# Two attention layers on one core: even batches and merged sums in layer 0, a direct first chunk, sums by query rows at the end

## The chip, the core and the metric

The kernel runs on one core of a Trainium2 chip, as one program. TensorE (PE, with its weight loads PEld), VectorE (DVE), ScalarE (ACT), GpSimd (POOL) and SyncE (SP) run beside each other, each through its own queue of instructions; transfers are issued from the queues of SP, ACT and POOL. The metric is device microseconds (us) of an execution.

## The reference

For each of 8 images of 64 channels and 64 x 64 points (N = 4096 points), two attentions follow each other:

```python
# layer 0
f = Wf @ x + bf;  g = Wg @ x + bg;  hh = Wh @ x + bh     # 8, 8 and 64 channels
beta = softmax(f.T @ g, axis=2)                          # 4096 x 4096
x = x + hh @ beta.T
# layer 1
xn = group_norm(x, 8 groups) * gamma + beta
q, k, v = split(w_qkv @ xn + b_qkv)
attn = softmax(q.T @ k / 8)
x = x + w_proj @ (v @ attn.T) + b_proj
```

All of it is float32.

## The kernel before

**Tiles.** An image stands in 128 rows: 64 channels of the first half of the points, 64 channels of the second half, 2048 columns each. A chunk `c` is 512 query points in each half, so an image has 4 chunks in each layer. For one chunk, a step `t` (16 of them) takes 128 key points, in both halves `p` of the keys, against both halves `h` of the queries. That is four score matmuls of 512 columns, here called units, which fill four of the eight PSUM banks; ScalarE takes the exponential into a tile `e` (128 x 2048; six buffers, tag `e` of `ppool`); TensorE multiplies `e` with the values (`weigh`), and VectorE adds `e` to `esum` (line 662), of which the softmax sums are made. A part is one key half of a step: two units. The softmax has no shift by a maximum: `bounds` looks at the end whether any sum left a safe range, and a flag read by the engines chooses a general path if one did.

**Layer 0.** f and g have 8 channels, each kept in four groups of 32 rows (one group for each pair of `h` and `p`), split into a high and a low part so that scores run in the float32r format. `project(k)` makes chunks 2k and 2k+1 of f and g at once: matmuls into one pair of banks, one activation that adds the bias (line 417), a cast into `high` (line 419), the split (line 422), and then 16 transfers on SP (line 432) that put the parts into their rows of f and g. `full` and `high` have one buffer each. `values(c)` makes the values of a chunk; outside of the loop VectorE copies them (line 298), within it ScalarE does.

**Layer 1.** Scores and weighing use 64 x 64 tiles of the array; a step is two pairs of banks. Group norm of image b's layer 1 and its q, k and values are made in earlier steps, as are f, g and values of later images.

**Order.** Chunks run in the order layer 0 of image 0, layer 0 of image 1, layer 1 of image 0, layer 0 of image 2, layer 1 of image 1, and so on. TensorE's order is exactly that of the program (`in_order`, line 137 is the matmul helper); on the other engines the framework orders by readiness, within given constraints (`issue_after`). Other work is put in by step number (`at_step`, `take`): work that takes a pair of banks (PAIR) or one spare bank (BANK) at most once in a batch.

**A batch of layer 0** is one turn of the loop: it scores as many units as there are free banks, 6, or 7 where the outer bank is free (`closed == 0`), 2 fewer where a PAIR is taken; then TensorE weighs parts whose exponentials were made in earlier batches. `due_part` lets it weigh up to 7 units' worth, 3.5 parts (a part can be cut into two halves of 256 columns), whatever the batch scored.

**The end of a chunk** (`finish`): the accumulated output is copied to `raw`. In layer 1, VectorE then adds the two halves of `esum` (line 312), and four matmuls with a block of ones (`sums`, some steps later) give the sums of 256 columns each; in layer 0 there is no such addition, the four matmuls have 512 columns, and the two halves are added after the sums were laid out (line 345). The sums go to `zs` (line 331), by four transfers to `zt` with 128 rows, through a reciprocal (line 347), to memory and back as a row for all channels (`r`), and `raw` is multiplied by it (line 366). The very last chunk has a short cut, `at_once`: two matmuls with ones give the sums in all rows, then a reciprocal of 128 x 512 (line 361), the product, the residual and `bounds` (lines 796 to 802).

**The start.** SP loads image 0 in four transfers of 64 rows; ACT's queue loads the weights of f and g in four transfers (line 169), POOL's the biases, `wh` and the small constants. All of `before()` of image 0 runs ahead of the loop: both projections with their 32 transfers, and the values of all four chunks. Then SP loads images 1 and 2, behind those transfers.

Of the kernel before, what the change touches and what calls it, by code (L numbers as in the profile page):

```python
# [9 lines left out]
F32 = mybir.dt.float32  # L10
# [58 lines left out]
def fast_path(  # L69
# [69 lines left out]
    x_tiles = {}  # L139

    def load_x(b):
        t = xpool.tile([P, NH], F32, tag="x", name=f"x_{b}")
        for k in range(2):
            for h in range(2):
                nc.sync.dma_start(
                    t[ts(h, C), ts(k, NH // 2)], x[b, :, ds(h * NH + k * (NH // 2), NH // 2)]
                )
        x_tiles[b] = t

    def both(name, src):  # L150
        t = const.tile([P, 1], F32, name=name)
        for h in range(2):
            nc.gpsimd.dma_start(t[ts(h, C), :], column(src))
        return t
# [6 lines left out]


    load_x(0)

    w1 = const.tile([P, 2, C8], F32, name="w1")
    fgb = const.tile([P, 1], F32, name="fgb")
    for h in range(2):
        for i, (w, bias) in enumerate(((WfT, bf), (WgT, bg))):
            nc.scalar.dma_start(w1[ts(h, C), i, :], w)  # L169
            nc.gpsimd.dma_start(  # L170
                fgb[ts(2 * h + i, 4 * C8), :], bias.unsqueeze(0).broadcast_to([4, C8])
            )
    wfg = const.tile([P, 2, 4, C8], F32, name="wfg")
# [3 lines left out]
    lane, low = const.tile([P, 1], I32, name="lane"), const.tile([P, 1], I32, name="low")  # L177
    nc.gpsimd.iota(lane, pattern=[[0, 1]], base=0, channel_multiplier=1)
    nc.vector.tensor_scalar(  # L179
        low, lane, 1, 2 * C8, op0=ALU.logical_shift_right, op1=ALU.bitwise_and  # L180
    )
    nc.vector.tensor_tensor(low, low, lane, op=ALU.bitwise_and)
    nc.vector.tensor_single_scalar(low, low, 1, op=ALU.logical_shift_right)
    nc.vector.tensor_tensor(low, low, lane, op=ALU.bitwise_xor)
    nc.vector.tensor_single_scalar(low, low, C8, op=ALU.bitwise_and)
    lowmask = const.tile([P, 1], F32, name="lowmask")
    nc.vector.tensor_scalar(lowmask, low, -1.0 / C8, None, op0=ALU.mult)
    wh = twice("wh", WhT)
# [20 lines left out]
    gavg = gavg.rearrange("p h g s -> p (h g s)")  # L209

# [7 lines left out]
    def layer1_constants():  # L218
# [20 lines left out]
        bet = both("bet", beta)  # L239
        wvt = const.tile([C, 2, C], F32, name="wvt")  # L240
# [957 lines left out]
```

## Time and profile before

| what | value |
|---|---|
| median of 3 runs | 3106.06 us (3105.13 to 3106.15) |
| profiled execution | 3105.83 us, span of its instructions 3104.1 us |
| TensorE busy | 3063.5 us (99%) |
| VectorE busy | 2506.6 us (81%) |
| ScalarE busy | 2045.5 us (66%) |
| mean granted TensorE clock | 0.996 of full speed |

The profile is of one execution. Times in it count from the first instruction of the span. A row of a group gives line, engine, operation, what it writes and reads, shapes and count, then busy time and mean duration of one in ns, then idle time of the engine ahead of them with what ended it. A row of the order of time gives start, duration, engine, line and what was done, with equal neighbours put together. One float32 matmul shows as two matmul records. TensorE's busy share tells little by itself, as its matmuls overlap; the time from the start of one row to the start of the next is the better measure.

### The profile page before, as it was taken

Reading aid. Unit: us, or ns where it says so; the run is one execution under the profiler, and the core shown is the slowest. Engines: PE = TensorE matmul, PEld = TensorE weight load, DVE = VectorE, ACT = ScalarE, POOL = GpSimd, SP = SyncE. Lnnn points to the kernel's source line nnn. Section 1 sums busy time; section 2 is a strip of 40 time slices with the busy share of each in tenths; the row PEclk is TensorE's granted clock in tenths of the full one; section 3 lists DMA queues with packets and bytes.
Section 4 is the critical chain, followed back from the end, with each engine's and each line's share of the span. In section 5 each row is a group of like instructions: output and inputs, shape, how many; then the busy total and the mean of one; then the engine's idle time right before and its main releaser. Section 6 shows DMA issues by size and latency. Waiting matters only on the chain.

```text
span 3104.1 us, 58905 instructions
## 1 busy us (share of the span) xinstructions
PE 3063.5 (99%) x25863; PEld 1122.5 (36%) x25863; DVE 2506.6 (81%) x1616; ACT 2045.5 (66%) x1976; POOL 16.7 (1%) x41
## 2 busy tenths in 40 slices
PE   7999999999999999999999999999999999999998
PEld 2333334333343333433334333343334333334433
DVE  6999876898768987689877997779977799776666
ACT  5788655786557865578555785558855587555554
POOL 2000000000000000000000000000000000000000
PEclk9999999999999999999999999999999999999999
DMA  3000010100101001010011000100001000000000
GB/s 84 22 8 11 18 39 15 32 1 15 39 21 26 1 15 39 22 25 1 15 39 25 21 1 19 42 19 21 1 25 35 19 8 2 14 22 15 10 13 12
DMA packets 61816, 63.16 MB, mean 20 GB/s; under 512 B 34944, under 2 KB 35024, under 8 KB 61552
## 3 DMA queue, kind: packets, MB, share of 16 engines
q1 hardware_dynamic: 60432, 59.16, 7.8%
q8 instruction: 204, 3.34, 0.5%
q14 instruction: 60, 0.49, 0.1%
q0 software_dynamic: 800, 0.15, 0.0%
q10 hardware_dynamic: 320, 0.01, 0.0%
HBM read 25.06 MB, written 8.65 MB: 11 GB/s over the span
## 4 chain that ended last, share of the span: by engine, by line
PE 96%; DVE 1%; ACT 1%; issue 1%; SPq 0%; DMA 0%; ACTq 0%; DVEq 0%
PE banks L137 96%; DVE esum_l L662 1%; ACT e_l L776 1%; SPq L432 0%; ACT e_l L736 0%; DMA w<-in_WgT_dram 0%; DMA x<-in_x_dram 0%; DVE vt_l L298 0%; DVE r_l L361 0%; DVE high_l L422 0%; DMA fg_l<-high_l 0%; ACTq L169 0%; DVE raw_l L366 0%; DVE esum_l L312 0%; ACT full_l L417 0%
## 5 line engine op out<-in xcount | busy, mean ns | idle before, releaser
L662 DVE TENSOR_TENSOR esum_l<-esum_l,e_l 128x2048 f32<-128x2048 f32 x896 | 2052.4, 2291 | 473.2 <-ACT e_l L736 414.5
L736 ACT ACTIVATE e_l<-banks 128x1024 f32<-128x1024 f32 x1024 | 992.8, 1021 | 802.8 <-PE banks L137 770.1
L137 PE MATMUL banks<-e_l,v_l 64*64 64x512 f32 (+1 forms) x8744 | 1098.5, 589 | 0.0
L776 ACT ACTIVATE e_l<-banks 128x2048 f32<-128x2048 f32 (+3 forms) x768 | 955.7, 1310 | 213.1 <-PE banks L137 207.9
L137 PE MATMUL banks<-kq_l 64*64 64x512 f32 (+1 forms) x8448 | 1010.2, 586 | 1.2 <-ACT e_l L776 1.1
L137 PE MATMUL banks<-e_l,vt_l 128*64 128x512 f32 (+1 forms) x3884 | 831.5, 567 | 0.0
L137 PEld LDWEIGHTS banks<-e_l,v_l 64*64 64x64 f32 (+1 forms) x8744 | 360.0, 133 | 576.0 <-issue 534.0
L137 PEld LDWEIGHTS banks<-kq_l 64*64 64x64 f32 (+1 forms) x8448 | 348.7, 134 | 579.3 <-issue 544.6
L137 PEld LDWEIGHTS banks<-e_l,vt_l 128*64 128x64 f32 x3884 | 254.3, 136 | 470.4 <-issue 457.0
L137 PE MATMUL banks<-fg_l 32*128 32x512 f32 x1792 | 220.2, 465 | 10.7 <-ACT e_l L776 5.7
L662 DVE TENSOR_TENSOR esum_l<-e_l,e_l 128x2048 f32<-128x2048 f32 x64 | 146.5, 2288 | 48.4 <-ACT e_l L736 35.9
L137 PEld LDWEIGHTS banks<-fg_l 32*128 32x128 f32 x1792 | 92.1, 183 | 219.4 <-ACT e_l L776 134.8
L137 PE MATMUL banks<-esum_l,ones 128*32 128x512 f32 (+2 forms) x508 | 55.2, 501 | 4.4 <-DVE esum_l L312 2.7
L568 DVE COPY raw_l<-banks 128x512 f32<-128x512 f32 x32 | 22.1, 692 | 31.3 <-PE banks L137 31.3
L366 DVE TENSOR_TENSOR raw_l<-raw_l,r_l 128x512 f32<-128x512 f32 x64 | 43.8, 684 | 0.0
L542 ACT ACTIVATE kq_l<-banks,qkb 128x512 f32<-128x512 f32 x64 | 40.6, 696 | 0.0
L312 DVE TENSOR_TENSOR esum_l<-esum_l 128x1024 f32<-128x1024 f32 x32 | 38.9, 1216 | 0.0
L137 PE MATMUL banks<-xn_l,wqk 64*64 64x512 f32 x256 | 33.4, 592 | 0.0
L331 ACT COPY zs_l<-banks 128x512 f32<-128x512 f32 (+1 forms) x63 | 30.9, 491 | 0.0
L137 PE MATMUL banks<-x,wfg 64*64 64x512 f32 x128 | 19.0, 640 | 9.7 <-DVE low L179 9.3
L137 PEld LDWEIGHTS banks<-wh,x 64*64 64x64 f32 x1024 | 22.0, 135 | 15.7 <-issue 13.3
L137 PEld LDWEIGHTS banks<-wvp,xn_l 64*64 64x64 f32 x1024 | 20.6, 134 | 16.8 <-issue 16.8
(89 smaller groups left out, 378.2 us busy)
## 6 DMA issues: line engine op xcount, KB each, us to landing
r_l<-recips SPq DMA_DIRECT2D x126, 128.0 KB, 2.9
fg_l<-high_l SPq DMA_DIRECT2D x224, 64.0 KB, 2.0
x<-in_x_dram SPq DMA_DIRECT2D x32, 256.0 KB, 5.2
kq_l<-kq_l SPq DMA_DIRECT2D x64, 128.0 KB, 2.3
out_dram<-raw_l SPq DMA_DIRECT2D x64, 128.0 KB, 2.4
kq_l<-high_l SPq DMA_DIRECT2D x32, 64.0 KB, 2.0
zt_l<-zs_l SPq DMA_DIRECT2D x128, 2.0 KB, 1.8
zt_l<-zs_l SPq DMA_DIRECT2D x124, 1.0 KB, 1.7
```

The costliest lines, as they stand in the source:

```text
L137: in_order(nc.tensor.matmul(*args, **kwargs))
L312: nc.vector.tensor_add(esum[:, 0], esum[:, 0], esum[:, 1])
L331: nc.scalar.copy(zs, z[:, 0:width])
L366: nc.vector.tensor_mul(raw, raw, r)
L542: nc.scalar.activation(self.parts[:, h, cols], ps[:, h, :], AF.Identity, bias=k1["qkb"][:, h : h + 1],)
L568: nc.vector.tensor_copy(raw, acc[0])
L662: added = nc.vector.tensor_add(esum, first if t == 1 else esum, e).ins
L736: nc.scalar.activation(e[:, p], both_ps[p], AF.Exp, scale=at.scale)
L776: nc.scalar.activation(e.rearrange("k p h n -> k (p h) n")[:, first_ : first_ + n_, :], banks[:, bank : bank + n_, :], AF.Exp, scale=at.scale,
```

## The change

Six edits. (1) `due_part` gets the room to weigh as the batch's own number of units: 7, 6, or 2 fewer. (2) Layer 0 adds the halves of `esum` on VectorE, right behind its last addition, and its sums have 256 columns as in layer 1. (3) The first chunk of image 0's f and g comes from matmuls with weights that already stand in the rows' layout (`direct`), so that it needs no transfer; the second chunk is projected alone, the third and fourth in step 1 of the loop, the values of chunks 1 to 3 in steps 2, 5 and 8. (4) Image 0 is loaded in three transfers of 128 rows, later images in two; the weights of f and g come in two transfers on ACT's queue, `wh` in one; images 1 and 2 are loaded from POOL's queue behind its small constants. (5) `fgb` and `lowmask` are put together by eight small copies on POOL. (6) In the last chunk the sums come as eight matmuls with `esum` as the weights, which puts queries in rows; the reciprocal is 128 x 8, and eight matmuls with the identity lay it out over the channels.

```diff
-
-    def load_x(b):
+    sent = []
+    def load_x(b, engine, cuts):
         t = xpool.tile([P, NH], F32, tag="x", name=f"x_{b}")
-        for k in range(2):
-            for h in range(2):
-                nc.sync.dma_start(
-                    t[ts(h, C), ts(k, NH // 2)], x[b, :, ds(h * NH + k * (NH // 2), NH // 2)]
-                )
+        for i, j in zip(cuts, cuts[1:]):
+            made = engine.dma_start(
+                t[:, i * CW : j * CW],
+                x[b].rearrange("c (h n) -> h c n", h=2)[:, :, i * CW : j * CW],
+            )
         x_tiles[b] = t
+        return made
     def both(name, src):
         t = const.tile([P, 1], F32, name=name)
         for h in range(2):
-            nc.gpsimd.dma_start(t[ts(h, C), :], column(src))
+            sent.append(nc.gpsimd.dma_start(t[ts(h, C), :], column(src)))
...
-    load_x(0)
-
     w1 = const.tile([P, 2, C8], F32, name="w1")
-    fgb = const.tile([P, 1], F32, name="fgb")
+    for i, w in enumerate((WfT, WgT)):
+        nc.scalar.dma_start(w1[:, i, :], w.unsqueeze(0).broadcast_to([2, C, C8]))
+    load_x(0, nc.sync, (0, 1, 2, 4))
+    bias2 = const.tile([P, 2], F32, name="bias2")
+    for i, bias in enumerate((bf, bg)):
+        nc.gpsimd.dma_start(
+            bias2[:, i : i + 1], bias.unsqueeze(0).broadcast_to([P // C8, C8])
+        )
+    direct = const.tile([P, 2, P], F32, name="direct")
+    nc.vector.memset(direct, 0.0)
     for h in range(2):
-        for i, (w, bias) in enumerate(((WfT, bf), (WgT, bg))):
-            nc.scalar.dma_start(w1[ts(h, C), i, :], w)
-            nc.gpsimd.dma_start(
-                fgb[ts(2 * h + i, 4 * C8), :], bias.unsqueeze(0).broadcast_to([4, C8])
-            )
+        rows = ts(h, C)
+        for i, at, n in ((0, h * C, 8), (1, h * 32, 4), (1, C + h * 32, 4)):
+            nc.vector.tensor_copy(
+                direct[rows, i, at : at + n * C8].rearrange("q (s c) -> q s c", c=C8),
+                w1[rows, i, :].unsqueeze(1).broadcast_to([C, n, C8]),
+            )
     wfg = const.tile([P, 2, 4, C8], F32, name="wfg")
     nc.vector.tensor_copy(wfg, w1.unsqueeze(2).broadcast_to([P, 2, 4, C8]))
     wfg = wfg.rearrange("p i s c -> p (i s c)")
-    lane, low = const.tile([P, 1], I32, name="lane"), const.tile([P, 1], I32, name="low")
...
-    wh = twice("wh", WhT)
+    nc.vector.tensor_tensor(low[:, 1:2], low[:, 0:1], low[:, 1:2], op=ALU.bitwise_xor)
+    lowmask2 = const.tile([P, 2], F32, name="lowmask2")
+    nc.vector.tensor_scalar(lowmask2, low, -1.0 / C8, None, op0=ALU.mult)
+    wh = const.tile([P, C], F32, name="wh")
+    nc.scalar.dma_start(wh, WhT.unsqueeze(0).broadcast_to([2, C, C]))
...
+    fgb, lowmask = const.tile([P, 1], F32, name="fgb"), const.tile([P, 1], F32, name="lowmask")
+    for j in range(2):
+        for i in range(2):
+            rows = ts(2 * j + i, 32)
+            nc.gpsimd.tensor_copy(fgb[rows, :], bias2[rows, i : i + 1])
+            nc.gpsimd.tensor_copy(lowmask[rows, :], lowmask2[rows, i : i + 1])
...
+        with tc.issue_after(sent[-1].ins):
+            for b in (1, 2):
+                load_x(b, nc.gpsimd, (0, 2, 4))
...
             raw = work.tile([P, CW], F32, tag="raw", bufs=4, name=f"raw_{n}")
+            last = index == 2 * B * NC - 1
+            if last:
+                with tc.issue_after(added):
+                    nc.vector.tensor_add(esum[:, 0], esum[:, 0], esum[:, 1])
             copied = self.total(raw, acc)
-            zt = small.tile([P, 2, QP], F32, tag="zt", bufs=5, name=f"zt_{n}")
-            width = CW if self.kind == 0 else CW // 2
-            if self.kind == 1:
-                with tc.issue_after(copied.ins):
+            zt = small.tile([P, QP], F32, tag="zt", bufs=4, name=f"zt_{n}")
+            width = CW // 2
+            if not last:
+                with tc.issue_after(copied.ins if self.kind == 1 else added):
                     nc.vector.tensor_add(esum[:, 0], esum[:, 0], esum[:, 1])
             r = None
...
-                zs = work.tile([P, CW], F32, tag="zs", bufs=1, name=f"zs_{n}")[:, 0:width]
+                zs = work.tile([P, width], F32, tag="zs", name=f"zs_{n}")
                 for h in range(2):
                     for i in range(2):
                         row = 32 * (2 * h + i)
-                        what = esum[:, i, h, :] if self.kind == 0 else esum[:, 0, h, ts(i, width)]
                         matmul(
-                            z[row : row + 32, 0:width], ones[:, 0:32], what,
+                            z[row : row + 32, 0:width], ones[:, 0:32], esum[:, 0, h, ts(i, width)],
                             start=True, stop=True, tile_position=(0, row),
                         )
                 nc.scalar.copy(zs, z[:, 0:width])
                 for h in range(2):
                     for i in range(2):
                         row = 32 * (2 * h + i)
-                        dst = zt[ts(h, C), i, :] if self.kind == 0 else zt[row : row + 32, 0, :]
-                        nc.sync.dma_start(dst, zs[row : row + 1, :])
+                        nc.sync.dma_start(zt[row : row + 32, :], zs[row : row + 1, :])
...
             def reciprocals():
-                zh = zt[:, 0, :]
-                if self.kind == 0:
-                    nc.vector.tensor_add(zh, zh, zt[:, 1, :])
                 rt = stash[:, ts(index, QP)]
-                nc.vector.reciprocal(rt, zh)
+                nc.vector.reciprocal(rt, zt)
                 broadcast()
...
             def at_once():
-                broadcast()
-                z = pair()[:, 0, :]
-                for h in range(2):
-                    matmul(z[ts(h, C), :], ones, esum[:, 0, h, :], start=True, stop=True)
-                nc.vector.reciprocal(r, z)
+                parts = [(h, k) for h in range(2) for k in range(TPC)]
+                z = pair()[:, 0, 0:QP]
+                for i, (h, k) in enumerate(parts):
+                    matmul(
+                        z[:, i : i + 1], esum[:, 0, h, ts(k, P)], ones[:, 0:1],
+                        start=True, stop=True,
+                    )
+                rt = zt
+                nc.vector.reciprocal(rt, z)
+                rows = work.tile([P, QP, C], F32, tag="full", bufs=1, name="rt_rows")
+                nc.vector.tensor_copy(rows, rt.unsqueeze(2).broadcast_to([P, QP, C]))
+                laid = pair()[:, 0, :]
+                for i, (h, k) in enumerate(parts):
+                    matmul(
+                        laid[ts(h, C), ts(k, P)], rows[:, i, :], ident, start=True, stop=True
+                    )
+                bounds(rt, 1)
+                nonlocal r
+                r = laid
                 result()
-                bounds(r, 1)
             def result():
                 nc.vector.tensor_mul(raw, raw, r)
                 self.residual(raw, c)
-            if index == 2 * B * NC - 1:
+            if last:
                 return (at_once,)
             return sums, reciprocals, result
...
-                self.project(0)
-
+                if self.b > 0:
+                    self.project(0)
+            if self.b == 0:
+                xt = x_tiles[0]
+                def first():
+                    begin()
+                    self.project_direct(0)
+                return [(-1, first, True), (-1, lambda: self.project(0, (1,)), True)] + [
+                    (1, lambda: self.project(1), True)
+                ] + [
+                    (
+                        (-1, 2, 5, 8)[c],
+                        lambda c=c: self.values(xt[:, ts(c, CW)], wh, c),
+                        True,
+                    )
+                    for c in range(NC)
+                ]
             at = (12, 28) if self.b == 1 else (17, 26)
             return [(at[0], begin, True), (at[1], lambda: self.project(1), True)] + [
...
-        def project(self, k):
+        def project_direct(self, c):
+            n = f"{self.name}_{c}"
+            cols = ts(c, CW)
+            ps = pair()
+            full = work.tile([P, 2, CW], F32, tag="full", bufs=1, name=f"full_{n}")
+            high = work.tile([P, 2, CW], F32R, tag="high", bufs=1, name=f"high_{n}")
+            for i, dst in enumerate((self.f, self.g)):
+                matmul(
+                    ps[:, i, :], direct[:, i, :], x_tiles[self.b][:, cols], start=True, stop=True
+                )
+                nc.scalar.activation(
+                    full[:, i, :], ps[:, i, :], AF.Identity, bias=bias2[:, i : i + 1]
+                )
+                nc.vector.tensor_copy(high[:, i, :], full[:, i, :])
+                nc.vector.scalar_tensor_tensor(
+                    dst[:, cols], high[:, i, :].bitcast(F32), lowmask2[:, i : i + 1],
+                    full[:, i, :], op0=ALU.mult, op1=ALU.add,
+                )
+        def project(self, k, js=(0, 1)):
             n = f"{self.name}_{k}"
             xt = x_tiles[self.b]
             ps = pair()
-            for j in range(2):
+            for j in js:
                 for h in range(2):
                     matmul(
                         ps[ts(j, C), h, :], wfg[ts(h, C), :], xt[ts(h, C), ts(2 * k + j, CW)],
                         start=True, stop=True,
                     )
             full = work.tile([P, 2, CW], F32, tag="full", bufs=1, name=f"full_{n}")
-            nc.scalar.activation(full, ps, AF.Identity, bias=fgb)
+            rows = slice(js[0] * C, P)
+            nc.scalar.activation(full[rows], ps[rows], AF.Identity, bias=fgb[rows, :])
             high = work.tile([P, 2, CW], F32R, tag="high", bufs=1, name=f"high_{n}")
-            nc.vector.tensor_copy(high, full)
+            nc.vector.tensor_copy(high[rows], full[rows])
...
             nc.vector.scalar_tensor_tensor(
-                split, high.bitcast(F32), lowmask, full, op0=ALU.mult, op1=ALU.add
-            )
-
-            for j in range(2):
+                split[rows], high[rows].bitcast(F32), lowmask[rows, :], full[rows],
+                op0=ALU.mult, op1=ALU.add,
+            )
+            for j in js:
                 cols = ts(2 * k + j, CW)
                 for h in range(2):
                     for p in range(2):
                         rows = ts(2 * h + p, 32)
                         for i, (dst, half) in enumerate(((self.f, h), (self.g, p))):
-                            self.sent = nc.sync.dma_start(
+                            nc.sync.dma_start(
                                 dst[rows, cols].bitcast(F32),
                                 split[ts(2 * j + i, 32), half, :].bitcast(F32),
                             )
...
-                load_x(self.b + 3)
+                load_x(self.b + 3, nc.sync, (0, 2, 4))
...
-    for _, u, _ in layers0[0].before():
-        u()
     makes = layer1_constants()
-    with tc.issue_after(layers0[0].sent.ins):
-        for b in (1, 2):
-            load_x(b)
     for i, u in enumerate(makes):
         at_step(NT + 2 + 2 * i, u)
+    for s, u, buffer in layers0[0].before():
+        if s < 0:
+            u()
+        else:
+            at_step(s, u, buffer)
...
-    def due_part(ready):
-
-
-        room, now_, left = 7, [], []
+    def due_part(ready, room):
+        now_, left = [], []
         for k, j, e, cols in ready:
             size = (cols.stop - cols.start) // (CW // 2)
             if seq[k][0].kind == 1 or room >= size:
...
             k, t = units[u][:2]
             now = k * NT + t
             due, taken = take(now + 1)
-            batch, left = due_part(ready)
+            wide = 7 if closed == 0 and taken != BANK else 6
+            batch, left = due_part(ready, wide - (2 if taken == PAIR else 0))
...
     def bounds(recip, i):
-        ok = work.tile(list(recip.shape), F32, tag="zs", bufs=1, name=f"ok_{i}")
+        ok = work.tile(list(recip.shape), F32, tag="raw", bufs=4, name=f"ok_{i}")
...
```

## The prediction

> **What bounds the kernel now.** I read the page first, then TensorE's order of time inside one layer-0 stage (image 2, 576 to 723 us), the busy time by stretches, and the order of time at both ends. Every number is in us unless marked.
>
> ```profile
> PE 3063.5 (99%) x25863; PEld 1122.5 (36%) x25863; DVE 2506.6 (81%) x1616; ACT 2045.5 (66%) x1976; POOL 16.7 (1%) x41
> ...
> L662 DVE TENSOR_TENSOR esum_l<-esum_l,e_l 128x2048 f32<-128x2048 f32 x896 | 2052.4, 2291 | 473.2 <-ACT e_l L736 414.5
> ...
> L312 DVE TENSOR_TENSOR esum_l<-esum_l 128x1024 f32<-128x1024 f32 x32 | 38.9, 1216 | 0.0
> ```
>
> TensorE is never without work, so what it issues sets the time. The merge that the change adds to layer 0 is already there for layer 1: line 312, 1.22 each.
>
> ```profile
> 586.78 0.64 PE L137 MATMUL banks<-esum_l,ones 128*32 128x256 f32 x8
> ...
> 593.46 0.73 PE L137 MATMUL banks<-fg_l 32*128 32x512 f32 x7
> 594.12 2.79 PE L137 MATMUL banks<-e_l,vt_l 128*64 128x512 f32 x12
> 596.85 0.97 PE L137 MATMUL banks<-fg_l 32*128 32x512 f32 x7
> 597.75 3.23 PE L137 MATMUL banks<-e_l,vt_l 128*64 128x512 f32 x16
> 600.91 0.73 PE L137 MATMUL banks<-fg_l 32*128 32x512 f32 x7
> ...
> 627.90 1.06 PE L137 MATMUL banks<-esum_l,ones 128*32 128x512 f32 x8
> 628.90 3.23 PE L137 MATMUL banks<-e_l,vt_l 128*64 128x256 f32 x16
> ```
>
> One batch is a row of scores (fg) and a row of weighing (e, vt). From start to start, scores take 0.66 whether 6 or 7; weighing takes 0.16 + 0.86 per part, 3 parts being 2.73 (x12) and 3.5 parts 3.16 (x16). At 596.85 the scores take 0.90: the batch before scored 7 but weighed 3 parts, TensorE came back early and ScalarE had not emptied the banks. The two sums rows are layer 1's (256 columns, 0.57 to the next row) and layer 0's (512 columns, 1.00).
>
> ```profile
> 576.50:722.90 146.40, 145.97 (x844) 49.36 (x842) 139.22 (x66) 122.40 (x103) 0.00 (x0) 1.00 0.05 12
> 723.00:957.60 234.60, 234.32 (x2384) 89.14 (x2384) 172.96 (x136) 132.61 (x143) 0.00 (x0) 1.00 0.11 26
> ```
>
> Columns: length, PE, PEld, DVE, ACT, POOL, clock. VectorE is busy 139.2 of 146.4 in layer 0; 54 hand-offs of 0.1 between its adds bring it to 144.6. It has 1.8 to spare there, and some 60 in layer 1.
>
> **Merged sums.** 32 sums fall from 1.00 to 0.57 on TensorE's path: 32 x 0.43 = 13.8 off. (The copies to zs fall from 0.595 to 0.383 on ScalarE, which is idle 24 per stage: nothing.) VectorE gets 31 more merges of 1.22 and loses 32 small adds of 0.16. Queued behind a merge are the next chunk's adds; who waits for those is ScalarE, which needs the e buffer of six tiles ago. In image 2's stage the least room between the end of that add and the start of the exponential is 4.3 (chunk 1), about 6 in chunk 3, 8.4 at the end. VectorE's lag would grow by three merges, 3.7, and by what TensorE gains, 2.5 by the stage's end; by chunk 3 that is 5.9 of 6. It just fits, and layer 1 gives it back. In images 0 and 1 (eight layer-0 chunks in a row, 23 to 340) VectorE idles 16 in all but only 0.9 from 145 to 260; there lag would grow by 3.3 of merges and 3.6 of TensorE's gain against 5.1 to 6 of room, and the group-norm steps of image 0, short VectorE operations that TensorE waits for, stand in it. Bounds: 0 to 16 lost; I take 3, since the room is nearly enough.
>
> **Even batches.** I walked the loop by its rules. Every stage of images 2 to 7 keeps 39 batches, so the 0.82 fixed per batch stays. In image 2's stage the waits above 0.66 sum to 2.6: 0.68 at the turn from layer 1 and eight of 0.21 to 0.29, each behind a batch that scored 7 and weighed 3 parts. In the new order the batches ahead of five of them (0.25, 0.21, 0.25, 0.24, 0.27) weigh 3.5; the other three and the turn stay: 1.2 saved, six times 7.3. From 82 to 340 the waits sum to 6.8 and larger ones (1.11, 1.06, 0.69, 0.68, 0.63) follow batches that weighed 2 to 3 parts; weighing in step with scoring leaves about 1.5: 5.3 saved. Bounds: 0 to 16 for both.
>
> **Start.** Before:
>
> ```profile
> 9.26 3.28 PE L137 MATMUL banks<-x,wfg 64*64 64x512 f32 x16 [9.26 <-DVE low L179]
> ...
> 14.49 31.07 SPq L432 DMA_DIRECT2D fg_l<-high_l  x29
> ...
> 21.33 1.63 PE L137 MATMUL banks<-fg_l 32*128 32x512 f32 x5 [2.91 <-DMA fg_l<-high_l]
> ...
> 22.97 5.56 ACT L776 ACTIVATE e_l<-banks 128x2048 f32<-128x2048 f32 x4 [7.27 <-PE banks L137]
> ```
>
> The last of four w transfers lands at 8.8, the second at 5.2. After, two transfers carry the same packets: 5.2 to 8.8, I take 6.3. Six small copies of 0.2 (line 248's size) give direct at 7.5. Two full matmuls of 512 columns follow: no such row, the nearest is four 64x64 tiles at 0.86 for both passes warm, twice that at the half clock of the start, so 1.7 each (0.9 if warm): 10.9. Activation 0.7 (line 542), half a cast 0.35, half a line 422 0.64, three hand-offs: f and g at 12.7. Beside that, chunk 1's projection and the first values end at 12.9, their copy 0.7: first scores at 13.7, not 21.33. From there to the first sums batch I count 16 batches weighing 42.5 parts: 16 x 0.82 + 42.5 x 0.86 + 5.2 (chunks 2 and 3's and image 1's projection, three values, layer-1 constants) = 54.9, plus 2 for the first exponentials and 1 at half clock: 71.6, against 82.02 and one unit (0.55) fewer, 9.9 gained if nothing waits. But chunk 2 of g still goes by transfers, needed 17 after the first scores, at 31. Its cast writes the buffer that chunk 1's eight transfers read: chunk 1's split ends at 15.6, 8 x 0.63 to issue and 2.0 to land is 22.7, cast 0.7, split 1.3 and up to one add of 2.4 between, then five issues and a landing, 5.8: 31 to 34. Loading images 1 and 2 now falls on GpSimd's queue behind its small transfers (0.52 each), from about 20 to 32, beside these. What that costs shows in the table of transfers (last column: us from issue to landing):
>
> ```profile
> fg_l<-high_l SPq DMA_DIRECT2D x224, 64.0 KB, 2.0
> ...
> w<-in_WfT_dram ACTq DMA_DIRECT2D x2, 2.0 KB, 5.6
> ```
>
> w's small transfers ran beside image 0's load, fg's mostly alone: up to 3 more. I take a wait of 3: 6.8 gained (2 to 10). [...] Nothing else waits for images 1 and 2 until about 44; their loading on SP held a projection at 51.5 (2.28 where 1.02 is usual). The eight copies for fgb and lowmask on GpSimd end long before the activation at 12; if not, they delay it by their own 1 to 2. wh moves to third place on ScalarE's queue, issued by 2.7 and wanted at 12; later loads give SP two issues in place of four: nothing for either.
>
> **End.** Now: last add 3087.38, merge, sums, a reciprocal of 128x512 (3.36), product, bounds on 512 columns, flag at 3098.37; then 5.7 of reading the flag and leaving, which hides the output's landing. After: merge first, 3088.6; eight sums, each like the 128x128 average over one column, 0.31 to the next row: 3091.1; reciprocal 0.2, copy 0.6, eight transposes of 128 columns at 0.21 (0.43 at half clock), 3094.0 to 3095.6; product and residual 1.5, flag at about 3096 to 3097.5: 0.9 to 2.4, I take 1.5. [...]
>
> **Sum.** 13.8 + 7.3 + 5.3 + 6.8 + 1.5 - 3.0 = 31.7. The profiled execution took 3105.83 (span 3104.1 and 1.7 around it), 0.2 under the median of 3106.06. So 3074.3.
>
> **Rivals.** (a) VectorE takes back part: the lag reaches the sixth buffer in chunk 3 of each stage and through images 0 and 1; each of six stages loses 1.2 to 2.5 and the start's pair 5 to 8 in place of 3: 3084 to 3096. For it: the 1.8 to spare. Against: VectorE waits for ScalarE again at 697 and 709, its lag there 0.03. (b) Slower: VectorE sets the pace of layer 0. Then all 25 merges that stand inside those stages (three in each of six, seven in the first pair) are paid at 1.22 and TensorE's gains there are void: +30.5, less 7 x 0.43 in layer 1, 6.8 and 1.5: +19, 3125. It decides once no room is left by the second chunk, which needs a merge to cost VectorE over 3. (c) The waits of 0.25 do not go, since ScalarE is late anyway, and g's transfers eat the start: 3074 + 12.6 + 6.8 = 3094; with (a) on top it ends within 0.2% of before.
>
> **How the numbers follow.** Forecast 0.68 (3064 to 3084), (a) and (c) 0.19, nothing measurable 0.05, (b) 0.08. 0.2% is 6.2, about what a measurement of this kernel can tell from no change. Range 3064 to 3096: the low end has every term at its better bound, the high end that of (a).
>
> **What would show it.** Layer-0 stages of images 2 to 7 at 144 instead of 146.4 to 147; sums rows all 0.57; scores rows of 0.9 down from nine to four per stage; first exponential near 14, first layer-0 sums near 75; VectorE's adds at a stage's end starting 5 to 7 behind their exponentials, with ScalarE never held by an add. It is wrong if ScalarE waits for VectorE's adds, if stages last 147 or more, or if the first scores wait past 17.

## The result, and the profile after

The changed kernel takes 3104.64 us (median of 4 runs, 3102.74 to 3105.92), the kernel before 3106.11 beside it (4 runs, 3105.13 to 3106.53): a ratio of 0.9995, 95% interval 0.9978 to 1.0013. No difference can be measured; 3074.3 was predicted, with 3064 to 3096 as the range. The profiled execution took 3104.7, span 3102.9, mean granted clock 0.993.

What was meant for the long run came. The engines' line, the adds, the merges on the page, and then TensorE's order of time in the layer-0 stage of image 2:

```profile
PE 3053.7 (98%) x26095; PEld 1136.5 (37%) x26095; DVE 2535.2 (82%) x1623; ACT 2042.0 (66%) x1978; POOL 19.8 (1%) x49
...
L737 DVE TENSOR_TENSOR esum_l<-esum_l,e_l 128x2048 f32<-128x2048 f32 x896 | 2052.3, 2291 | 462.7 <-ACT e_l L811 402.9
...
L338 DVE TENSOR_TENSOR esum_l<-esum_l 128x1024 f32<-128x1024 f32 x63 | 76.8, 1219 | 0.8
```

```profile
603.36 0.64 PE L137 MATMUL banks<-esum_l,ones 128*32 128x256 f32 x8
603.93 2.80 PE L137 MATMUL banks<-e_l,vt_l 128*64 128x512 f32 x12
...
625.14 0.73 PE L137 MATMUL banks<-fg_l 32*128 32x512 f32 x7
625.80 3.23 PE L137 MATMUL banks<-e_l,vt_l 128*64 128x256 f32 x16
```

A sums row costs 0.57 to the next row (603.36 to 603.93), and a batch that scores 7 now weighs 3.5 parts. The two stages as stretches (length, PE, PEld, DVE, ACT, POOL busy, clock, DMA share, GB/s):

```profile
592.45:737.10 144.65, 144.24 (x876) 50.61 (x873) 137.94 (x67) 121.76 (x103) 0.00 (x0) 1.00 0.04 12
737.10:971.41 234.31, 234.03 (x2386) 89.23 (x2384) 179.05 (x135) 132.38 (x143) 0.00 (x0) 1.00 0.10 26
```

The stage of 146.4 to 147 is 144.6 now; from one image to the next it is 378.96 instead of 381.76, six times 2.8 = 16.8 off. The last stage is 471.0 instead of 472.4. But layer 0 of image 2 begins at 592.45, where it began at 575.89: 16.6 were lost ahead of it. TensorE's order of time at the start:

```profile
10.49 2.04 PE L137 MATMUL banks<-x,direct 128*128 128x512 f32 x2 [10.49 <-DMA x<-in_x_dram]
14.59 2.07 PE L137 MATMUL banks<-x,direct 128*128 128x512 f32 x2 [2.06 <-DVE direct L181]
16.59 1.97 PE L137 MATMUL banks<-x,wfg 64*64 64x512 f32 x4
23.19 1.13 PE L137 MATMUL banks<-wh,x 64*64 64x64 f32 x32 [4.62 <-DMA wh<-in_WhT_dram]
27.77 0.80 PE L137 MATMUL banks<-fg_l 32*128 32x512 f32 x4 [3.45 <-DVE fg_l L473]
```

Image, weights and `wh` are late one after the other, and the first scores come at 27.8, not at 13.7. The stretches, and the loads of images 1 and 2 in the table of transfers (last column: us to landing), say why:

```profile
5.00:10.00 5.00, 0.00 (x0) 0.00 (x0) 0.00 (x0) 1.28 (x1) 1.71 (x7) 1.00 0.13 42
10.00:15.00 5.00, 2.45 (x3) 0.91 (x4) 0.72 (x5) 0.69 (x1) 0.00 (x0) 1.00 0.14 49
15.00:20.00 5.00, 3.57 (x6) 0.38 (x5) 0.00 (x0) 0.69 (x1) 0.00 (x0) 1.00 0.13 52
```

```profile
x<-in_x_dram POOLq DMA_DIRECT2D x4, 512.0 KB, 17.2
```

The share is a mean over 16 engines, so 0.13 adds up to 2.1 of them busy. Before, the same bytes came at a share of 0.94 and 171 to 226 GB/s, done by 8:

```profile
2.50:5.00 2.50, 0.00 (x0) 0.00 (x0) 0.00 (x0) 0.00 (x0) 2.41 (x6) 1.00 0.94 226
5.00:8.00 3.00, 0.00 (x0) 0.00 (x0) 0.00 (x0) 0.00 (x0) 2.80 (x10) 1.00 0.94 171
```

The second loss stands between 226 and 260, in the first pair of layer-0 images. All engines:

```profile
243.14 0.38 PE L137 MATMUL banks<-mv_l,gavg 128*128 128x1 f32 x2
...
245.13 7.08 DVE L737 TENSOR_TENSOR esum_l<-esum_l,e_l 128x2048 f32<-128x2048 f32 x3
245.75 0.95 PE L137 MATMUL banks<-kq_l 32*128 32x512 f32 x4
252.25 0.16 DVE L557 COPY mu_l<-banks 128x1 f32<-128x1 f32 x1
...
252.46 0.79 PE L137 MATMUL banks<-kq_l 32*128 32x512 f32 x2 [5.76 <-DVE mu_l L557]
```

The group means were made at 243.5, but the copy that empties their banks (line 557) stands in VectorE's queue behind three adds. The scores that come next want those banks and wait 5.76. In the kernel before, the copy came 2.5 after its matmuls instead of 8.7, and no scores waited for it:

```profile
231.88 0.38 PE L137 MATMUL banks<-mv_l,gavg 128*128 128x1 f32 x2
...
234.80 0.16 DVE L482 COPY mu_l<-banks 128x1 f32<-128x1 f32 x1
```

### The profile page after: what moved, and what is told of

It reads as the page before. It is cut to its first block, busy times and chain, and to the rows that moved or that the text cites. A ratio compares the mean times of both kernels' runs of the same rounds, so it can differ in the third digit from the quotient of the medians.

```text
span 3102.9 us, 59400 instructions
## 1 busy us (share of the span) xinstructions
PE 3053.7 (98%) x26095; PEld 1136.5 (37%) x26095; DVE 2535.2 (82%) x1623; ACT 2042.0 (66%) x1978; POOL 19.8 (1%) x49
## 4 chain that ended last, share of the span: by engine, by line
PE 92%; DVE 4%; issue 2%; ACT 1%; DMA 0%; SPq 0%; POOL 0%; DVEq 0%; ACTq 0%; POOLq 0%
PE banks L137 92%; DVE esum_l L737 3%; ACT e_l L811 0%; ACT e_l L852 0%; DMA fg_l<-high_l 0%; SPq L507 0%; DVE esum_l L338 0%; DVE vt_l L320 0%; DVE high_l L496 0%; DVE raw_l L401 0%; DMA zt_l<-zs_l 0%; DVE x L530 0%; DVE esum_l L332 0%; POOL bias L173 0%; SPq L360 0%
## 5 line engine op out<-in xcount | busy, mean ns | idle before, releaser
L137 PE MATMUL banks<-e_l,v_l 64*64 64x512 f32 (+2 forms) x8772 | 1100.2, 588 | 0.0
L137 PEld LDWEIGHTS banks<-e_l,vt_l 128*64 128x64 f32 x4060 | 267.6, 137 | 473.5 <-issue 453.5
L137 PE MATMUL banks<-fg_l 32*128 32x512 f32 x1792 | 211.5, 461 | 10.9 <-DMA fg_l<-high_l 4.5
L737 DVE TENSOR_TENSOR esum_l<-e_l,e_l 128x2048 f32<-128x2048 f32 x64 | 146.4, 2288 | 13.9 <-ACT e_l L811 9.8
L338 DVE TENSOR_TENSOR esum_l<-esum_l 128x1024 f32<-128x1024 f32 x63 | 76.8, 1219 | 0.8
L137 PE MATMUL banks<-esum_l,ones 128*32 128x256 f32 x504 | 40.7, 395 | 1.6 <-DVE vt_l L320 1.6
L137 PE MATMUL banks<-wh,x 64*64 64x64 f32 x1024 | 22.8, 225 | 5.3 <-DMA wh<-in_WhT_dram 4.6
L137 PEld LDWEIGHTS banks<-wvp,xn_l 64*64 64x64 f32 x1024 | 20.6, 134 | 16.8 <-issue 16.8
L526 ACT COPY raw_l<-banks 128x512 f32<-128x512 f32 x32 | 19.0, 595 | 11.6 <-PE banks L137 11.4
## 6 DMA issues: line engine op xcount, KB each, us to landing
x<-in_x_dram POOLq DMA_DIRECT2D x4, 512.0 KB, 17.2
```

The source lines that it names most:

```text
L137: in_order(nc.tensor.matmul(*args, **kwargs))
L338: nc.vector.tensor_add(esum[:, 0], esum[:, 0], esum[:, 1])
L526: nc.scalar.copy(raw, acc[0])
L737: added = nc.vector.tensor_add(esum, first if t == 1 else esum, e).ins
```

## The experiments

Each time is a median beside runs of the kernel before on the same chip (3105.4, 3105.7, 3106.6 and 3105.7 in the four groups), and each ratio is to those.

**The form of the transfers.** `e1_halves`, `e2_halves_x` (images alone) and `e3_halves_w` (weights alone):

```diff
-            made = engine.dma_start(
-                t[:, i * CW : j * CW],
-                x[b].rearrange("c (h n) -> h c n", h=2)[:, :, i * CW : j * CW],
-            )
+            for h in range(2):
+                made = engine.dma_start(
+                    t[ts(h, C), i * CW : j * CW], x[b, :, ds(h * NH + i * CW, (j - i) * CW)]
+                )
...
-        nc.scalar.dma_start(w1[:, i, :], w.unsqueeze(0).broadcast_to([2, C, C8]))
+        for h in range(2):
+            nc.scalar.dma_start(w1[ts(h, C), i, :], w)
...
-    nc.scalar.dma_start(wh, WhT.unsqueeze(0).broadcast_to([2, C, C]))
+    for h in range(2):
+        nc.scalar.dma_start(wh[ts(h, C), :], WhT)
```

> The changed kernel with every transfer of 128 rows (image loads, weights of f and g, wh) issued as two of 64 rows again, in the same queues and order; all else as changed. Theory A (form of the transfers): the changed kernel's loads, whose access pattern begins with a dimension of 2, keep only two of the 16 DMA engines busy (share 0.13, some 50 GB/s, from 5 to 25 us), and this holds everything at the start back. Then the DMA share between 4 and 8 us is above 0.8, the weights land by 9, the first scores come at 15 to 16 instead of 27.8, the first layer-0 sums at 78 to 82 instead of 98.0, and the time is 16 to 20 under the changed kernel's: 3084 to 3090. Rival B (the new chain itself: waiting weights, six small copies, two full matmuls, activation, split, masks): the first scores stay past 22 and the time stays at 3098 or more. Theory C (VectorE's lag in images 0 and 1): whatever the start does, TensorE still waits 5 or more for a group-norm step of image 0 between 230 and 260, as it did for 5.8.

> Only the image loads are in halves of 64 rows; the weights of f and g and wh keep the form that begins with a dimension of 2. Theory A: the image no longer fills the two engines that the weights need, so they land by 9 or earlier, though each on two engines; first scores at 15 to 17, within 2 of the run with all in halves, time 3084 to 3092. If the weights' form is what costs (rival), the first scores stay past 22 and the time is above 3096.

> Only the weights of f and g and wh are in halves; the image loads keep the form that begins with a dimension of 2. Theory A: the image still comes at some 50 GB/s, so its first chunk of 256 KB needs 5 us and its second 5 more; the first scores come at 18 to 22, and the loading of images 1 and 2 still stands in front of f's and g's transfers at 45 to 58 (wait of 5.8 in the changed kernel). Time 3094 to 3101. If the weights' form were the whole cost (rival), it ends with the run with all in halves.

Measured: 3086.15 (0.9936, 0.9923 to 0.9950), 3086.77 (0.9936, 0.9922 to 0.9950) and 3100.13 (0.9983, 0.9974 to 0.9992). In the run with all in halves, two stretches and then TensorE's first and first scores' rows:

```profile
4.00:6.00 2.00, 0.45 (x1) 0.48 (x2) 0.49 (x3) 1.28 (x1) 1.73 (x8) 1.00 0.95 216
6.00:8.00 2.00, 2.00 (x3) 0.65 (x3) 0.62 (x4) 0.36 (x1) 0.81 (x4) 1.00 0.81 242
```

```profile
5.55 3.75 PE L137 MATMUL banks<-x,direct 128*128 128x512 f32 x4 [5.55 <-DMA x<-in_x_dram]
...
14.85 0.80 PE L137 MATMUL banks<-fg_l 32*128 32x512 f32 x4 [3.44 <-DVE fg_l L475]
```

The same bytes move at 216 to 242 GB/s, and the first scores are 12.9 earlier. Layer 0 of image 2 begins at 574.68 instead of 592.45: the form alone cost 17.8. The image is what matters: with it in halves the weights may stay in the changed form, while with the weights alone in halves the image's third transfer still holds TensorE at 25.9 for 4.7. In the changed kernel the loads of the start, whose pattern begins with a dimension of 2, ran at a share of 0.13, about two engines' worth; as halves of 64 rows they ran at 0.81 to 0.95. What other sizes of that dimension would do is not shown. Transfers of 128 rows were had here only through a leading 2, and the kernel with them measured 18.5 worse (3104.64 against 3086.15).

As theory C had it, the wait for the group means stayed: 5.8 in the table of waits of this run.

**Merges in the first pair.** `e4_unmerged01` is `e1_halves` with

```diff
             width = CW // 2
-            if not last:
+            merged = self.kind == 1 or self.b > 1
+            width = CW // 2 if merged else CW
+            if merged and not last:
```

> As the run with all in halves, but in layer 0 of images 0 and 1 alone the halves of esum are not merged by VectorE: the sums have 512 columns there (1.00 instead of 0.57, eight times, 3.4 more for TensorE) and a small add of 0.16 follows. Theory D (the merges overfill VectorE in images 0 and 1): VectorE's lag behind the exponentials stays under 7, the wait of 5.8 for a group-norm step near 245 falls under 2, and with the half clock behind it some 8 go, so the time is 4 to 5 under the run with all in halves. Rival (VectorE is as late without the merges, for TensorE and ScalarE run faster there than before): the wait stays over 4 and the time is 2 to 4 above it.

Measured: 3082.38 (0.9926, 0.9912 to 0.9939), 3.8 under `e1_halves`, where 4 to 5 were expected, although eight sums cost 0.43 more each. Its own table of waits:

```profile
PE banks L137 <- DVE fg_l L482: 3.4, 1, 3.4
PE banks L137 <- DMA fg_l<-high_l: 1.7, 2, 1.2
...
PE banks L137 <- DVE mu_l L566: 1.2, 1, 1.2
```

The wait falls from 5.8 to 1.2, as theory D expected.

**Single parts on the kernel before.** `e5_before_merged`, `e6_before_even`, `e7_before_both`:

```diff
-            if self.kind == 1:
-                with tc.issue_after(copied.ins):
+            if True:
+                with tc.issue_after(copied.ins if self.kind == 1 else added):
...
-        room, now_, left = 7, [], []
+        now_, left = [], []
...
-            batch, left = due_part(ready)
+            wide = 7 if closed == 0 and taken != BANK else 6
+            batch, left = due_part(ready, wide - (2 if taken == PAIR else 0))
```

> The kernel before with merged sums in layer 0 alone (the last chunk too), all else as before. Gain on TensorE: 32 sums at 0.57 instead of 1.00, 13.8 (one group-norm batch of the changed kernel showed 1.01, so 13.3). Theory D (the merges overfill VectorE in images 0 and 1, also without the new start and without even batches): a wait of 5 or more for a group-norm step of image 0 appears between 225 and 250, as in the changed kernel and in the run with halves, and half clock behind it; the time is 3098 to 3101. Rival (the overload needs TensorE to run as even batches make it run): no wait over 2 there, time 3091 to 3094.

> The kernel before with even batches alone. As predicted (six stages at 1.2 less, waits of the first pair down from 6.8 to 1.5): 12.6 off, 3093. From the comparison of the two traces: stages of images 2 to 7 were 2.4 shorter in all, of which four merged sums explain 1.7, so 0.7 to 1.1 per stage for even batches, 4 to 7, and 3 to 5 in the first pair: 3094 to 3098. Rival (the waits move to other batches): no change, 3105.

> The kernel before with merged sums and even batches, its old start and old end. If the two add, less the wait for the group-norm step (7 with its half clock) where theory D holds: 3086 to 3090. Theory E (the new start gives next to nothing even with its transfers in halves): this run then stands within 2 of the run with all in halves (3086.2), which has the new start and the new end on top. As predicted the start would be worth 6.8 and the end 1.5, so this run would be 8 above it: 3094.

Measured: 3097.37 (0.9974, 0.9963 to 0.9984), 3096.34 (0.9970, 0.9959 to 0.9981), 3088.63 (0.9945, 0.9931 to 0.9958). Image to image the three take 380.05, 380.67 and 378.96 against 381.76: 1.71, 1.09 and 2.80 off, so in the steady part the two add. In the first pair they do not: layer 0 of image 2 begins at 577.38, 570.96 and 576.56, against 575.89. The waits for the group-norm steps of image 0, from the tables of waits of merged, even and both, in this order:

```profile
PE banks L137 <- DVE mu_l L480: 2.6, 1, 2.6
```

```profile
PE banks L137 <- DVE ve_l L491: 0.6, 1, 0.6
```

```profile
PE banks L137 <- DVE mu_l L480: 6.4, 1, 6.4
```

Merges alone make 2.6, which lies between theory D and its rival, as the time does; with even batches, which alone bring TensorE on by 4.9 in the first pair, it is 6.4. From even to both the first pair grows by 5.6, though its eight sums are 3.4 shorter: the merges cost 9.0 there. Theory E nearly holds: with both parts but the old start and end, the kernel is 2.5 above `e1_halves`, and layer 0 of image 2 begins 1.9 later; the start was to bring 6.8.

**Can the wait be had out of the way?** `e12_halves_mu` is `e1_halves`, `e11_all_merged_mu` the fastest kernel below with merges everywhere, both with

```diff
-                nc.vector.tensor_copy(mu, ps[:, 0, 0:1])
+                nc.scalar.copy(mu, ps[:, 0, 0:1])
```

> The run with all transfers in halves (3086.2; merges everywhere), with the copy of the group means out of the banks made by ScalarE instead of VectorE. Theory H (TensorE waits 6.8 there because that copy stands behind three adds of 2.3 in VectorE's queue and so holds the pair of banks): the wait at 228 falls under 1, the half clock after it goes too, and the time is 3079 to 3081. Rival (VectorE is simply too late in images 0 and 1: ScalarE has 0.09 of room left before it needs a buffer that an add still reads): ScalarE then waits for adds, and at least 4 of the 7 come back elsewhere: 3083 or more.

> The fastest run so far (3076.1, sums unmerged in images 0 and 1) with the merges in all images again and the copy of the group means on ScalarE. Theory H: eight sums at 0.57 instead of 1.00 (3.4) and the wait of 1.15 for the group means go: 3071.5 to 3073. Rival (as in the run before): VectorE's lag holds ScalarE in images 0 and 1, 3076 or more.

Measured: 3084.76 (0.9928, 0.9912 to 0.9945) and 3078.91 (0.9911, 0.9894 to 0.9928). The second is 2.8 worse than without merges in the first pair (`e10_all` below), but not all of it is the merges' price: its first layer-0 sums come at 75.3 against 72.7, before any merge of layer 0 can matter (its clock fell there, as shown below), and these 2.6 are part of the 4.3 by which layer 0 of image 2 begins later (568.0 against 563.7). The wait went to the next group-norm step, as the table of waits of the first shows:

```profile
PE banks L137 <- DVE v_l L562: 4.5, 1, 4.5
```

So theory H named the place, and not the cause: with the copy (5.8) out of the way, the next short operation that VectorE owes TensorE there stood behind its adds (4.5). An add held ScalarE for 0.6 once, so the rival's mechanism was wrong too, though its number was right.

**What is left of the start.** `e8_gfirst`, `e9_early`, `e13_behind`, `e14_early_behind` are `e4_unmerged01` with one or two of three edits, and `e10_all` has all three (the mask block is moved, not changed):

```diff
+            every = [(j, h, p, i) for j in js for h in range(2) for p in range(2) for i in range(2)]
+            if self.b == 0:
+                every.sort(key=lambda e: -e[3])        # g first
...
+    masked = nc.vector.tensor_scalar(lowmask2, low, -1.0 / C8, None, op0=ALU.mult)
+    with tc.issue_after(masked.ins):                  # early: then the copies into direct
...
+                with tc.issue_after(self.split.ins):  # early: copy of the first values
...
+                def others():                         # behind: images 1 and 2 on SP
+                    self.project(1)
+                    for b in (1, 2):
+                        load_x(b, nc.sync, (0, 2, 4))
```

> The run with halves and unmerged sums in images 0 and 1, and in the start: masks made first on VectorE and the copy of the first values behind the split of the first chunk (the trace of that run shows VectorE's queue standing until 11.1 at that copy, and GpSimd's until 13.0 at the mask); the transfers of g ahead of those of f in image 0; images 1 and 2 loaded from SP behind those transfers. If these queues are what is left of the start's loss: first scores at 11.5 to 12.5 instead of 14.5, the wait of 3.0 for g's second half falls under 1, and the time is 3 to 6 under 3082.4: 3076 to 3079. Rival (the rest is the first exponentials' own pace, TensorE at half clock): 3081 or more.

> The run with halves and unmerged sums in images 0 and 1 (3082.4), with the one edit that in image 0 the transfers of g go ahead of those of f. Theory F (the wait of 3.0 at 34.5 is g's transfers): the fourth transfer of g's next chunk is issued fourth instead of eighth, 1.8 to 2.4 earlier, the wait falls to 0.6 to 1.2, half clock behind it shrinks, time 3078.5 to 3080.5. Theory G (it is the pause of TensorE before the first scores, 3.4, and the half clock that follows it, that cost most of what the run with all of the start's edits, 3076.1, had gained): under 1.5 gained here, 3081 or more.

> The same run (3082.4) with the other edit alone: masks first on VectorE, the copy of the first values behind the split of the first chunk; transfers in the old order, images 1 and 2 still from GpSimd. Theory G: TensorE's pause before the first scores falls from 3.4 to 0.8, the clock is not halved after it, and 4 to 5.5 of the 6.3 come from this edit: 3077 to 3078.5. Theory F: only the waits for transfers count, 1 to 2 gained: 3080.5 or more.

> The run with halves and unmerged sums in images 0 and 1 (3082.4), with images 1 and 2 loaded from SP behind the transfers of chunks 2 and 3 of f and g, as in the kernel before, instead of from GpSimd. Theory I (2 MB of images ahead of g's transfers on the same 16 engines make the wait at 34.5): the wait of 3.0 falls to 1.2 to 2, the half clock behind it goes, time 3078.5 to 3080.5. Rival (the wait is the order of the transfers on SP's queue, which this leaves): 3081.5 or more.

> The run before this one with the masks and the split of the first chunk ahead of the first values' copy. Alone that edit brought nothing: GpSimd, freed sooner, issued the images' loads at 19.7 instead of 24.2, and a wait of 5.8 for f's and g's transfers stood at 24.9. Theory I: with the images behind, it brings what it was made for (a pause of TensorE of 0.8 instead of 3.4 before the first scores, no half clock): 2.5 to 4.5 under the run with the images behind alone, 3076 to 3077.5. Rival: no more than 1 under it.

Measured: all three 3076.08 (0.9905, 0.9890 to 0.9920), g first 3079.83 (0.9915, 0.9899 to 0.9932), early 3082.22 (0.9923, 0.9906 to 0.9939), the images' place 3081.46 (0.9921, 0.9905 to 0.9938), early with that place 3079.36 (0.9912, 0.9896 to 0.9929).

The images did not go where the edit put them. SP's queue did not keep the order in which they are written: with the early masks it issued all eight of their transfers between 6.0 and 11.1, ahead of f's and g's; in `e13_behind` five went ahead and three stood at 24.6. In `e14_early_behind`, where all of them were issued by 11 and the DMA share was 0.01 or less from 24 to 32, the batch that wants g's next chunk still waits 3.4 in all. So their traffic is not what makes that wait, and theory I falls; with g first it is 2.1 (`e8_gfirst`: the time is where theory F had put it, the wait is longer than the 0.6 to 1.2 expected), with all three edits 1.2. In `e9_early` GpSimd, freed sooner, issued the images from 17.7 to 21.7, on top of chunk 1's transfers (the 19.7 of a later expectation is a misreading), and TensorE waited there:

```profile
28.37 0.66 PE L137 MATMUL banks<-fg_l 32*128 32x512 f32 x2 [3.01 <-DMA fg_l<-high_l]
30.61 0.79 PE L137 MATMUL banks<-fg_l 32*128 32x512 f32 x3 [1.58 <-DMA fg_l<-high_l]
```

Theory G thus fell for that edit by itself: 0.2 gained. With the images ahead it brings 2.1, a little less than was expected, and g first another 3.3; a run with the images ahead and nothing else was not made, so the share of each is known only in this order. Both are of the size of the spread: the runs of `e13_behind` go from 3079.1 to 3085.7, those of `e14_early_behind` from 3077.1 to 3080.8, those of `e10_all` from 3075.4 to 3076.9.

The time of `e10_all` is in the range of its expectation, but its start is not: the first scores come at 14.57 and not at 11.5 to 12.5. The early masks and copies stand ahead of the copies into `direct` in VectorE's queue, so that the direct matmuls, which in `e4_unmerged01` wait for the image, now wait for VectorE. The rows of `e4_unmerged01`, then of `e10_all`:

```profile
5.55 3.75 PE L137 MATMUL banks<-x,direct 128*128 128x512 f32 x4 [5.55 <-DMA x<-in_x_dram]
```

```profile
7.96 3.78 PE L137 MATMUL banks<-x,direct 128*128 128x512 f32 x4 [7.96 <-DVE direct L192]
```

What differs after that is the clock. The first scores' row and two stretches of `e4_unmerged01`, then of `e10_all`:

```profile
14.45 0.80 PE L137 MATMUL banks<-fg_l 32*128 32x512 f32 x4 [3.44 <-DVE fg_l L482]
```

```profile
14.00:18.00 4.00, 2.59 (x12) 0.60 (x12) 2.11 (x3) 2.93 (x2) 3.84 (x11) 0.50 0.07 20
18.00:22.00 4.00, 3.30 (x44) 1.77 (x42) 0.97 (x2) 3.42 (x4) 4.00 (x9) 0.50 0.25 76
```

```profile
14.57 0.51 PE L137 MATMUL banks<-fg_l 32*128 32x512 f32 x4 [0.80 <-DVE vt_l L322]
```

```profile
14.00:18.00 4.00, 2.03 (x16) 0.59 (x16) 2.49 (x3) 3.65 (x3) 1.17 (x2) 1.00 0.93 197
18.00:22.00 4.00, 3.66 (x51) 1.56 (x53) 1.91 (x1) 3.15 (x4) 3.60 (x7) 1.00 0.29 73
```

Both score first at 14.5, but after a pause of 3.44 the granted clock was 0.50 up to 22, after one of 0.80 it was 1.00. The first layer-0 sums come in batches at 80.5 and 72.7. By these two rows the length of the pause would set the clock, but three other runs do not agree: `e9_early`, `e11_all_merged_mu` and `e14_early_behind` have the early edit too and no pause of TensorE above 1.2 before the stretch once it had begun at 7.9, and their clock still fell. In `e9_early` it was 0.58 from 18 to 20 and 0.57 from 20 to 22. The first scores' row of `e14_early_behind`, its stretch, and the one of `e11_all_merged_mu`:

```profile
14.29 0.50 PE L137 MATMUL banks<-fg_l 32*128 32x512 f32 x4 [1.05 <-DVE vt_l L322]
```

```profile
18.00:22.00 4.00, 3.68 (x40) 1.45 (x40) 1.93 (x1) 2.51 (x3) 3.35 (x7) 0.59 0.27 77
```

```profile
18.00:22.00 4.00, 3.83 (x40) 1.71 (x40) 2.08 (x1) 2.36 (x3) 3.59 (x7) 0.57 0.33 86
```

So the full clock of `e10_all` is not shown to be the work of "early", and what decides it with such short pauses stays open.

`e10_all` beats both kernels: the one before by 29.6, and the changed one by 28.6 across the groups.

## Why the prediction was wrong

| term | predicted | measured | from |
|---|---|---|---|
| merged sums on TensorE | -13.8 | -13.7 | steady part of merged alone, 6 x 1.71, and 8 x 0.43 |
| even batches, images 2 to 7 | -7.3 | -6.5 | even alone, 6 x 1.09 |
| even batches, first pair | -5.3 | -4.9 | even alone, 570.96 against 575.89 |
| VectorE's lag | +3.0 | +9.0 | even to both, 5.6 + 3.4 |
| start, transfers in halves | -6.8 | -1.9 | 574.68 in halves, 576.56 in both |
| form of the transfers | 0 | +17.8 | 592.45 after, 574.68 in halves |
| end | -1.5 | -1.4 | last stage, 471.0 against 472.4 |

The measured column sums to -1.6; the medians differ by 1.5.

**The step that failed** is the load of image 0 in its new form: a term of the start that the prediction put at nothing, without a reason. It took only the weights' transfers as the limit, "After, two transfers carry the same packets: 5.2 to 8.8, I take 6.3", had `direct` at 7.5, and put `wh`, wanted at 12, at "nothing". That holds where the image comes in halves: in `e2_halves_x` the two weight transfers have the changed form still, the second has landed at 6.7, `direct` is complete at 7.3, and nothing waits for `wh`. In the changed kernel the image, loaded at a DMA share of 0.13, has its first chunk there only at 10.49, the second transfer of w lands at 14.0, and `wh` at 23.2. VectorE's copies into `direct`, in the changed kernel and then in `e2_halves_x`:

```profile
13.99 0.54 DVE L181 COPY direct<-w 64x32 f32<-64x32 f32 x4 [9.57 <-DMA w<-in_WgT_dram]
```

```profile
6.74 0.54 DVE L181 COPY direct<-w 64x32 f32<-64x32 f32 x4 [2.31 <-DMA w<-in_WgT_dram]
```

So the term was +17.8 and not 0. The part counted the issues of the new transfers and never asked how many of the 16 engines they would keep busy: a share of 0.13 for them, 0.94 for the transfers before.

**The start's own gain** was mis-sized as well. In halves the first scores came at 14.85 for 13.7, and the batch that wants g's next chunk lost 2.87 for 3. What fell short lies between: 65.8 from the first scores to the first sums' batch, where 57.9 and 3 were counted. Other waits there take 4.3 (1.09, 0.85, 1.05 and 1.32; 2 allowed), and half clock about 4 (1 allowed; an estimate, half of the 7.5 that TensorE was busy up to 24 at 0.50, as a sums row took 1.01 for 0.57 at that clock in the changed kernel), which follows the pause of 3.44: VectorE's queue stood at the copy of the first values until 11.5, with the casts and the masks behind it. The copies for fgb and lowmask did not "end long before the activation at 12"; they waited for those masks and held it.

**VectorE's lag** had the right place and the wrong measure. I priced it by the room between an add and the exponential that needs its buffer. That room did shrink, to 0.09 at 245.1, and yet held ScalarE for no more than 0.6. What cost was TensorE's order: a pair of banks is empty only when VectorE reaches a small copy, and that copy stands behind as many adds as the lag is long. The text named those steps and gave them no price of their own: three adds are 7.1.

Right were the terms of the steady part: stages of 144.6 for 144, sums rows of 0.57 (one of 1.01 at half clock), waits above 0.66 in image 2's stage of 1.6 in all instead of 2.6 (1.2 saved was predicted), VectorE some 7 behind at the stage's end for 5 to 7, ScalarE not held there. The end's number is right, its path only in part: the flag was ready at 3095.3, a little sooner than forecast, but from there to the end of the span it took 7.6, where it had been 5.7; what that time waits for is not shown. Rival (a) had VectorE take back 5 to 8 in the first pair. It was 6.5 with the new start (574.68 in `e1_halves` against 571.54 in `e4_unmerged01`, and the 3.4 of the sums) and 9.0 with the old one; but no stage of images 2 to 7 lost anything. (b) would have needed VectorE to pace every stage. (c) had g's transfers eat the start; in halves they cost just what the forecast gave them.

## What to carry to other kernels

Before a transfer is re-shaped, look at the first dimension of its access pattern, and then, as the check, at the DMA share of the first microseconds: with a leading 2 it was 0.13 here, about two engines of sixteen, and in halves of 64 rows 0.81 to 0.95. Where an engine has nearly no room, ask which of its short operations another engine waits for in program order: here the lag was paid there (5.76 at the group means), while an add held ScalarE for no more than 0.6. And measure the parts of a bundled change one by one: here 16.8 of gain stood behind 17.8 of loss, and the total said "nothing".

## What was not expected of the hardware

The loads with a leading 2 moved 42 to 52 GB/s from 5 to 20, at a DMA share of 0.13 to 0.14, and GpSimd's queue was no way around it (512 KB landed in 17.2, against 6.1 for 256 KB in halves). Pauses of TensorE of 3.44 (`e1_halves`), 4.62 and 5.76 (the changed kernel) were each followed by a granted clock of 0.50, where it had been 1.00, so a wait cost more than its length: with the 5.8 for the group means, the next weighing of three parts took 4.38 instead of 2.73. But short pauses were no guarantee of the full clock: with none above 1.2, it was 1.00 in one run and 0.57 to 0.59 in three, in the same stretch of 4.
